# Attention weights on one Trainium2 core: turned tiles in two buffers with transfers of their own

## The chip, the cores and the metric

The kernel runs on one core of one Trainium2 chip. The times are device microseconds (us). The core's engines work beside each other, each through its own instructions in order: TensorE (PE in the profile, its weight loads PEld) multiplies matrices, VectorE (DVE), ScalarE (ACT) and GpSimd (POOL) work on elements, and SyncE (SP) issues the transfers (DMAs) of this stage. They wait for one another through semaphores.

## The reference

The input is 16 sequences of 512 tokens of width 256, in float32. Three layers follow one another, each added to its input: half of a feed-forward block with experts, a causal attention of 16 heads with rotary positions, and half of the same feed-forward block again. The change is in the attention:

```python
q = _rope(q.reshape(b, s, H, DQK).transpose(0, 2, 1, 3))
k = _rope(k.reshape(b, s, H, DQK).transpose(0, 2, 1, 3))
scores = jnp.einsum('bhqd,bhkd->bhqk', q, k) * (1.0 / np.sqrt(DQK))
scores = jnp.where(causal[None, None], scores, -jnp.inf)
probs = jax.nn.softmax(scores, axis=-1)
out = jnp.einsum('bhqk,bhkd->bhqd', probs, v)
return out.transpose(0, 2, 1, 3).reshape(b, s, H * DV) @ Wo + bo
```

A head has 64 columns in q, k and v.

## The kernel before

**Units.** A unit is one sequence and one group of four heads (`HG`): 16 x 4 = 64 units, in this order. The loop over `u` (L1207) is a pipeline over units: in one turn it makes the sums and the output projection of unit `u`, finishes the weights of unit `u + 1` (`old`), makes scores and exponentials of unit `u + 2` (`new`), and the queries and keys of unit `u + 3`.

**Tiles.** The 512 tokens are four tiles of 128. Scores are causal, so tile i of the queries has i + 1 blocks of 128 keys: ten blocks a head. `place` (L1020) says where they lie: tile 3 (four blocks) and tile 2 (three) in one buffer `pr0`, tiles 1 and 0 (two and one) in `pr1`.

**From scores to sums.** `scores` (L1038) lets TensorE fill one PSUM bank a head. `exps` (L1061) takes a head and a tile at a time: VectorE masks and finds the row minimum of the negated scores (L1073), ScalarE takes the exponential and the row sum (L1077). `scaled` (L1080) takes the reciprocal on VectorE and multiplies on GpSimd (L1085). Now the weights have queries on the partitions, and the sums over keys need keys there. So each 128x128 block is turned in two steps. First `turn` (L1088) transposes its sixteen 32x32 squares on VectorE from `pr` into `sq` (L1100); `turn_most(j)` does the three first key blocks of tiles 3 and 2 for head j, `turn_corner` the last block of tile 3 for all heads, `turn_tile(1)` and `turn_tile(0)` the other two tiles. Then `move` (L1119) carries the squares to other partitions: for each quarter of 32 partitions that is a source (`q`) and each that is a target (`k`) one transfer, 16 in all, from `sq` to `prT` (L1127), issued on SP. Each is 32 partitions x 5120 bytes. `sums` (L1149) multiplies: for two heads side by side and for each key tile t one matmul a head over all query tiles i >= t at once (L1158). To make that one contiguous piece, `first` (L1019) gives the place of the first block of each key tile. ScalarE copies the result out of PSUM with the bias (L1169), `leave` (L1171) projects it (L1176), and VectorE adds it to the stream (L1182).

**Order.** Within the attention the instructions of VectorE, ScalarE, GpSimd and SP, and of TensorE in the whole kernel, run in the order in which the program names them; nothing rearranges them. `sq`, `prT`, `pr0`, `pr1` and the values `v` have one buffer each, so a unit writes one only after the unit before has been read. PSUM has eight banks, given out in turn. In one turn of the loop VectorE's order is: reciprocals of tiles 1 and 0, `turn_most(1)`, `turn_most(2)`, more reciprocals, `turn_most(3)`, the corner, tile 1, tile 3 of `new` for head 0, tile 0 (and then SP's 16 transfers), the rest of tiles 3 and 2, the addition to the stream, the rotation of queries and keys (L994), `turn_most(0)` of `new`, and tiles 1 and 0 of `new`.

**Other transfers on SP.** Once per sequence (four units) a sequence that comes later is normalized, its squares turned on VectorE (L961), stored to memory as `away` (L964), and loaded back in two times eight transfers (`land`, L970), which stand at the start of a turn, ahead of the `move`. At the fourth head group the output of a sequence is stored (L1184).

**First and last unit.** Unit 0 and unit 63 are turned by TensorE instead (`turn_at_once`, L1129).

## Time and profile before

| | us |
|---|---|
| median of 3 runs (2309.47 to 2314.15) | 2309.89 |
| profiled execution, its own time | 2317.09 |
| span of its instructions | 2315.4 |
| PE busy | 2254.7 (97%) |
| DVE busy | 1761.6 (76%) |
| ACT busy | 1158.1 (50%) |
| POOL busy | 1068.6 (46%) |

The granted clock of TensorE was 0.995 of full speed in the profiled execution. The attention runs from about 449 us to 1925 us of the span; before and after it the feed-forward blocks run.

How the rows are read: a group of instructions has its line of the kernel, engine and operation, the tile that it writes and those that it reads, the shape, how many there were, busy time and mean length in ns, and the idle time of the engine just before them with what ended it. A row of waits has who waited, for whom, the total, how many times and the longest. A row of one line's instructions has minimum, median and maximum length in ns. A row of the timeline has start, length, engine, line, operation and count.

### The profile page before, as it was taken

The numbers are of one execution on the slowest core, as the hardware profiler recorded it, in microseconds if no ns is written. First come the engines' busy times: TensorE is split into PE (matmuls) and PEld (weight loads), VectorE is DVE, ScalarE is ACT, GpSimd is POOL, SyncE is SP. The second block draws the span as 40 slices with busy tenths as digits, with TensorE's granted clock in tenths as the row PEclk, the third lists the DMA queues.
The fourth block names the chain that finished last, engine by engine and source line by source line (L and its number), as shares of the span: only waits on it lengthen the run. The fifth ranks groups of instructions, "written<-read, shape, count | busy, mean of one in ns | idle before, by whom it ended". The sixth has DMA issues, their size and how long they took to land. (4 is left out here: it accounts for less than half of the span.)

```text
span 2315.4 us, 52884 instructions
## 1 busy us (share of the span) xinstructions
PE 2254.7 (97%) x19544; PEld 1488.2 (64%) x19544; DVE 1761.6 (76%) x4678; ACT 1158.1 (50%) x3296; POOL 1068.6 (46%) x1695
## 2 busy tenths in 40 slices
PE   7999999999999999999999999999999999998999
PEld 4764488566666666666666666666666666764588
DVE  5742298788889898989898988989888875432387
ACT  5753243455555555556464545555555555532233
POOL 2210054565566556565656565656556542210043
PEclk9999999999999999999999999999999999999999
DMA  6839851055556465554655554646455543739734
GB/s 209 261 112 403 339 140 55 7 131 121 130 127 147 110 148 130 122 140 111 146 129 129 128 140 111 158 97 160 120 132 130 124 115 112 237 138 404 305 116 140
DMA packets 221929, 359.52 MB, mean 155 GB/s; under 512 B 99876, under 2 KB 159848, under 8 KB 213480
## 3 DMA queue, kind: packets, MB, share of 16 engines
q1 hardware_dynamic: 220812, 355.34, 55.3%
q8 instruction: 155, 2.54, 0.5%
q14 instruction: 102, 0.84, 0.1%
q10 hardware_dynamic: 860, 0.81, 0.1%
HBM read 156.29 MB, written 37.22 MB: 84 GB/s over the span
## 5 line engine op out<-in xcount | busy, mean ns | idle before, releaser
L1085 POOL TENSOR_SCALAR pr<-pr,ars 128x512 f32<-128x512 f32 (+3 forms) x1024 | 524.1, 532 | 575.0 <-DVE ars L1082 573.8
L1077 ACT ACTIVATE pr<-pr,amn 128x512 f32<-128x512 f32 (+3 forms) x1024 | 561.8, 550 | 219.6 <-DVE amn L1073 215.2
L1100 DVE STREAM_TRANSPOSE sq<-pr 128x768 f32<-128x768 f32 x434 | 384.5, 918 | 130.1 <-DMA prT<-sq 106.7
L1073 DVE CUSTOM_DVE_ANT_0 pr<-p_as,causal 128x512 f32<-128x512 f32 (+2 forms) x768 | 308.6, 457 | 7.0 <-PE p_as L1054 5.8
L1054 PE MATMUL p_as<-k,q 32*64 32x448 f32 (+3 forms) x8192 | 307.3, 414 | 0.0
L1158 PE MATMUL p_av<-prT,v 128*64 128x512 f32 (+3 forms) x2048 | 291.5, 437 | 10.1 <-ACT pr L1077 2.0
L1013 ACT COPY v<-p_v 128x512 f32<-128x512 f32 x128 | 74.6, 585 | 451.3 <-PE p_v L1010 451.3
L1158 PEld LDWEIGHTS p_av<-prT,v 128*64 128x64 f32 x2048 | 161.1, 137 | 139.6 <-issue 92.7
L1176 PE MATMUL p_ay<-wo,aoT 128*128 128x256 f32 x1024 | 238.6, 386 | 4.1 <-DVE amn L1073 3.0
L1010 PE MATMUL p_v<-wv,ahT 128*128 128x256 f32 x1024 | 231.6, 379 | 0.7 <-DVE x L1182 0.7
L988 PE MATMUL p_q<-ahT,wq 128*128 128x512 f32 x512 | 230.6, 593 | 0.2 <-ACT ahT L949 0.2
L1054 PEld LDWEIGHTS p_as<-k,q 32*64 32x64 f32 x8192 | 201.8, 131 | 45.0 <-issue 26.2
L988 PE MATMUL p_k<-ahT,wk 128*128 128x512 f32 x512 | 230.3, 592 | 0.0
L1176 PEld LDWEIGHTS p_ay<-wo,aoT 128*128 128x128 f32 x1024 | 189.2, 190 | 62.2 <-DVE amn L1073 37.0
L1010 PEld LDWEIGHTS p_v<-wv,ahT 128*128 128x128 f32 x1024 | 194.5, 190 | 53.8 <-issue 23.7
L1077 ACT ACTIVATION_READ_ACCUMULATOR pr<-pr,amn 128x1 f32 x1024 | 192.0, 187 | 0.0
L988 PEld LDWEIGHTS p_k<-ahT,wk 128*128 128x128 f32 x512 | 97.3, 190 | 122.0 <-issue 106.9
L988 PEld LDWEIGHTS p_q<-ahT,wq 128*128 128x128 f32 x512 | 97.0, 190 | 95.7 <-issue 78.6
L1073 DVE CUSTOM_DVE_ANT_1 pr<-p_as,causal 128x384 f32<-128x384 f32 x256 | 130.2, 546 | 0.0
L1169 ACT ACTIVATE aoT<-p_av,bcol 128x128 f32<-128x128 f32 (+1 forms) x384 | 117.1, 391 | 9.9 <-PE p_av L1158 9.9
L584 PE MATMUL p_ds<-hT,qk 128*128 128x512 f32 x256 | 118.8, 609 | 2.1 <-ACT hT L159 2.1
L811 PE MATMUL p_cy<-vw,catT 128*128 128x256 f32 x512 | 120.8, 379 | 0.0
(179 smaller groups left out, 3358.0 us busy)
## 6 DMA issues: line engine op xcount, KB each, us to landing
prT<-sq SPq DMA_DIRECT2D x992, 160.0 KB
w<-in_e_W_dram SPq DMA_DIRECT2D x64, 1024.0 KB
w<-in_e_Wg_dram SPq DMA_DIRECT2D x32, 1024.0 KB
out_dram<-x SPq DMA_DIRECT2D x64, 256.0 KB
awaya<-sqa SPq DMA_DIRECT2D x25, 512.0 KB
atT<-awaya SPq DMA_DIRECT2D x100, 128.0 KB
xl<-in_attn_x_dram SPq DMA_DIRECT2D x16, 512.0 KB
xl<-out_dram SPq DMA_DIRECT2D x16, 512.0 KB
```

The source lines that it names most:

```text
L584: nc.tensor.matmul(psc, qk[:, k, c * P:(c + 1) * P], hT[:, k, :], start=(k == 0), stop=(k == NC - 1))
L811: nc.tensor.matmul(py[:, t * D:(t + 1) * D], atT[:, c, t * P:(t + 1) * P], vws[b][:, c, :], start=(c == 0), stop=(c == NC - 1))
L988: nc.tensor.matmul(pq, self.w[:, k, at:at + P], hTs[self.b][:, k, :], start=(k == 0), stop=(k == NC - 1))
L1010: nc.tensor.matmul(pv[:, t * 256:(t + 1) * 256], hTs[b][:, k, (t0 + t) * P:(t0 + t + 1) * P], wv[:, k, hg * HG * DQ:(hg + 1) * HG * DQ], s ...
L1054: nc.tensor.matmul(banks[j][half * H:(half + 1) * H, at:at + wh], q[n][rows, q0:q0 + H], k[n][rows, :wh], start=(n == 0), stop=(n == 1))
L1073: nc.vector.tensor_tensor_reduce(out=by_block(self.at(i, j)), in0=by_block(banks[j][:, at:at + w]), in1=mask(i), scale=-1.0 / math.sqrt(DQ ...
L1077: nc.scalar.activation(self.at(i, j), self.at(i, j), AF.Exp, bias=self.mn[:, i, j:j + 1], scale=-1.0, accum_out=self.rs[:, i, j:j + 1])
L1085: nc.gpsimd.tensor_scalar(self.at(i, j), self.at(i, j), self.rs[:, i, j:j + 1], 1.0, ALU.mult, ALU.mult)
L1100: nc.vector.transpose(view(self.sq, j * blocks * SQ + dst[0] * SQ, [(blocks * SQ, nh)] + [(s * SQ, n) for s, (_, n) in zip(dst[1:], of)] + ...
L1158: nc.tensor.matmul(po[j * DQ:(j + 1) * DQ, :].rearrange("d (a f) -> d a f", a=NSQ)[:, :, t * SQ:], vs[u][:, t, head * DQ:(head + 1) * DQ], ...
L1169: nc.scalar.activation(dst[:, odd, to], src[:, odd, of], AF.Identity, bias=bcol[:, r:r + 1])
L1176: nc.tensor.matmul(py[:, t * D:(t + 1) * D], oTs[u][:, pair, (t0 + t) * P:(t0 + t + 1) * P], wo[:, hg * (HG // 2) + pair, :], start=(pair ...
```

## The change

The turned weights lie in two buffers, as the weights before turning do: `sq0` and `prT0` for tiles 3 and 2 (seven blocks a head), `sq1` and `prT1` for tiles 1 and 0 (three blocks). Each has a `move` of its own of 16 transfers: 32 partitions x 3584 bytes, and 32 partitions x 1536 bytes. The space is the same in all. Three further things go with it:

- Within a `move` the target quarters come in the order 0, 2, 1, 3 in place of 0, 1, 2, 3.
- All of `turn_most` and the corner of a unit stand one turn of the loop earlier than three of the four and the corner did, ahead of the exponentials of its tiles 1 and 0; `move(0)` stands at the start of the next turn, ahead of the scaling of tiles 1 and 0. `turn_tile(1)`, `turn_tile(0)` and `move(1)` come behind tile 3 of `new` for heads 0 and 1.
- `sums` has six pieces in place of four: for key tile t the queries of tiles 3 and 2 from the first buffer (t = 0 to 3), and then those of tiles 1 and 0 from the second (t = 0 and 1). The columns are the same in all.

```diff
-        blocks = NT * (NT + 1) // 2
-        first = [0, 4, 8, 7]
+        blocks = (7, 3)
+        where = ([(2, 0), (3, 0), (2, 1), (3, 1), (2, 2), (3, 2), (3, 3)], [(0, 0), (1, 0), (1, 1)])
+        pieces = [(0, t, max(t, 2), NT - max(t, 2)) for t in range(NT)] + [(1, t, t, 2 - t) for t in range(2)]
...
-                if heads[0] == 0 and which == 0 and len(of) == 2:
-                    self.sq = ap.tile([P, NSQ, HG, blocks * SQ], F32, tag="sq", name=f"sq{self.nm}")
+                n = blocks[which] * SQ
+                if self.sq[which] is None:
+                    self.sq[which] = ap.tile([P, NSQ, HG, n], F32, tag=f"sq{which}", name=f"sq{which}_{self.nm}")
...
-            def move(self):
-                prT = prTs[self.u] = ap.tile([P, NSQ, HG, blocks * SQ], F32, tag="prT", name=f"prT{self.nm}")
+            def targets(self, tag, which):
+                if which == 0:
+                    prTs[self.u] = [None, None]
+                n = blocks[which] * SQ
+                prT = prTs[self.u][which] = ap.tile([P, NSQ, HG, n], F32, tag=f"{tag}{which}",
+                                                    name=f"prT{which}_{self.nm}")
+                return prT
+
+            def move(self, which):
+                prT, sq = self.targets("prT", which), self.sq[which]
                 for n in range(NSQ):
-                    for k in range(NSQ):
+                    for k in (0, 2, 1, 3):
                         q = (k + n) % NSQ
-                        nc.sync.dma_start(prT[k * SQ:(k + 1) * SQ, q, :, :], self.sq[q * SQ:(q + 1) * SQ, k, :, :])
+                        nc.sync.dma_start(prT[k * SQ:(k + 1) * SQ, q, :, :], sq[q * SQ:(q + 1) * SQ, k, :, :])
...
-            for t in range(NT):
-                n = NT - t
+            for one, (which, t, i, n) in enumerate(pieces):
+                at = where[which].index((i, t))
                 for j in range(2):
                     head = pair * 2 + j
                     nc.tensor.matmul(
-                        po[j * DQ:(j + 1) * DQ, :].rearrange("d (a f) -> d a f", a=NSQ)[:, :, t * SQ:],
+                        po[j * DQ:(j + 1) * DQ, :].rearrange("d (a f) -> d a f", a=NSQ)[:, :, i * SQ:(i + n) * SQ],
                         vs[u][:, t, head * DQ:(head + 1) * DQ],
-                        prTs[u][:, :, head, first[t] * SQ:(first[t] + n) * SQ],
-                        start=(t == 0), stop=(t == NT - 1))
+                        prTs[u][which][:, :, head, at * SQ:(at + n) * SQ],
+                        start=(one == 0), stop=(one == len(pieces) - 1))
...
                 elif old:
+                    old.move(0)
                     old.scaled((1, 0), slice(0, HG // 2))
-                    old.turn_most(1)
-                    old.turn_most(2)
                     old.scaled((1, 0), slice(HG // 2, HG))
-                    old.turn_most(3)
-                    old.turn_corner()
-                    old.turn_tile(1)
                 if new:
                     new.scores((3,))
                     new.scores((2,))
-                    new.exps((3,), slice(0, 1))
+                    new.exps((3,), slice(0, 2))
                 if old and 0 <= u < nu - 2:
+                    old.turn_tile(1)
                     old.turn_tile(0)
-                    old.move()
-                if new:
-                    new.exps((3,), slice(1, 2))
+                    old.move(1)
...
                     new.scores((1, 0))
                     if u + 3 < nu:
-                        new.turn_most(0)
+                        for j in range(HG):
+                            new.turn_most(j)
+                        new.turn_corner()
                     new.exps((1, 0))
```

`turn_at_once` (units 0 and 63) fills both buffers in the same way, with the same ten PSUM banks.

More of the change, by code (lines that the diff above doesn't have):

```diff
@@ L1030, in __init__ @@
                 self.rs = small.tile([P, NT, HG], F32, tag="ars", name=f"ars{self.nm}")
-                self.pr = [None, None]
+                self.pr, self.sq = [None, None], [None, None]
                 self.banks = {}
@@ L1088, in turn @@
             def turn(self, which, heads, of, src, dst):
-                if heads[0] == 0 and which == 0 and len(of) == 2:
-                    self.sq = ap.tile([P, NSQ, HG, blocks * SQ], F32, tag="sq", name=f"sq{self.nm}")
-                pr = self.pr[which]
+                n = blocks[which] * SQ
+                if self.sq[which] is None:
+                    self.sq[which] = ap.tile([P, NSQ, HG, n], F32, tag=f"sq{which}", name=f"sq{which}_{self.nm}")
+                pr, sq = self.pr[which], self.sq[which]
                 def view(x, at, dims):
@@ L1098, in turn @@
                 j, nh = heads
-                step = (7, 3)[which] * P
+                step = blocks[which] * P
                 nc.vector.transpose(
-                    view(self.sq, j * blocks * SQ + dst[0] * SQ,
-                         [(blocks * SQ, nh)] + [(s * SQ, n) for s, (_, n) in zip(dst[1:], of)]
-                         + [(HG * blocks * SQ, NSQ), (1, SQ)]),
+                    view(sq, j * n + dst[0] * SQ,
+                         [(n, nh)] + [(s * SQ, m) for s, (_, m) in zip(dst[1:], of)]
+                         + [(HG * n, NSQ), (1, SQ)]),
                     view(pr, j * step + src * P,
@@ L1107, in turn_most @@
             def turn_most(self, j):
-                self.turn(0, (j, 1), [(3, 2), (1, 3)], 0, (2, 1, 3))
+                self.turn(0, (j, 1), [(3, 2), (1, 3)], 0, (0, 1, 2))
             def turn_corner(self):
-                self.turn(0, (0, HG), [], 6, (first[3],))
+                self.turn(0, (0, HG), [], 6, (6,))
             def turn_tile(self, i):
                 if i:
-                    self.turn(1, (0, HG), [(1, 2)], 1, (1, 3))
+                    self.turn(1, (0, HG), [(1, 2)], 1, (1, 1))
@@ L1129, in turn_at_once @@
             def turn_at_once(self, tag, vector):
-                prT = prTs[self.u] = ap.tile([P, NSQ, HG, blocks * SQ], F32, tag=tag, name=f"prT{self.nm}")
-                where = {first[t] + i - t: (i, t) for i in range(NT) for t in range(i + 1)}
-                per = S // P
-                for g in range(HG * blocks // per):
-                    pt = ps(f"p_prT{self.nm}_{g}")
-                    for n in range(per):
-                        j, at = divmod(g * per + n, blocks)
-                        i, t = where[at]
-                        nc.tensor.transpose(pt[:, n * P:(n + 1) * P], self.at(i, j)[:, t * P:(t + 1) * P], ident)
-                    dst = prT.rearrange("p a h f -> p a (h f)")[:, :, g * per * SQ:(g + 1) * per * SQ]
-                    dst = dst.rearrange("p a (n x) -> p a n x", n=per)
-                    src = pt.rearrange("p (n a x) -> p a n x", n=per, a=NSQ)
-                    if g in vector:
-                        nc.vector.tensor_copy(dst, src)
-                    else:
-                        nc.scalar.copy(dst, src)
+                per, done = S // P, 0
@@ new lines, in turn_at_once @@
+                for which in range(2):
+                    prT = self.targets(tag, which)
+                    for g in range(HG * blocks[which] // per):
+                        pt = ps(f"p_prT{self.nm}_{done}")
+                        for n in range(per):
+                            j, at = divmod(g * per + n, blocks[which])
+                            i, t = where[which][at]
+                            nc.tensor.transpose(pt[:, n * P:(n + 1) * P], self.at(i, j)[:, t * P:(t + 1) * P], ident)
+                        dst = prT.rearrange("p a h f -> p a (h f)")[:, :, g * per * SQ:(g + 1) * per * SQ]
+                        dst = dst.rearrange("p a (n x) -> p a n x", n=per)
+                        src = pt.rearrange("p (n a x) -> p a n x", n=per, a=NSQ)
+                        if done in vector:
+                            nc.vector.tensor_copy(dst, src)
+                        else:
+                            nc.scalar.copy(dst, src)
+                        done += 1
```

## The prediction

> **What bounds the kernel now.** I read the page's busy shares and groups first, then the waits, then one line's issues, then the timeline of one unit.

> ```profile
> PE 2254.7 (97%) x19544; PEld 1488.2 (64%) x19544; DVE 1761.6 (76%) x4678; ACT 1158.1 (50%) x3296; POOL 1068.6 (46%) x1695
> ...
> L1100 DVE STREAM_TRANSPOSE sq<-pr 128x768 f32<-128x768 f32 x434 | 384.5, 918 | 130.1 <-DMA prT<-sq 106.7
> ...
> L1158 PE MATMUL p_av<-prT,v 128*64 128x512 f32 (+3 forms) x2048 | 291.5, 437 | 10.1 <-ACT pr L1077 2.0
> ```

> TensorE is the bound. The wait that the change is aimed at is VectorE's: 106.7 us in 52 waits, because the turn of head 0 (L1100) may not overwrite `sq` before the transfers of the unit before have read it.

> One line's issues, on the queue SP:

> ```profile
> L1127 SPq DMA_DIRECT2D prT<-sq x992: 507/590/1704, 460.3 to 1899.5; - x199
> L970 SPq DMA_DIRECT2D ahT<-away x224: 303/449/1736, 546.9 to 1787.1; - x112
> ```

> Issuing one transfer holds SP for 590 ns at the median. A unit has 16 of them (992 in 62 units).

> The timeline of one unit, by engine (start, length, then the work; S is the start of its sums, 1038.93):

> ```profile
> 1038.93 4.53 PE L1158 MATMUL p_av<-prT,v 128*64 128x512 f32 x32
> 1043.39 0.22 PE L1047 MATMUL p_as<-blank 32*64 32x64 bf16 x4
> ...
> 1045.18 0.21 PE L1047 MATMUL p_as<-blank 32*64 32x64 bf16 x3
> ...
> 1046.46 3.72 PE L1176 MATMUL p_ay<-wo,aoT 128*128 128x256 f32 x16
> ```

> ```profile
> 1033.92 5.37 SPq L970 DMA_DIRECT2D ahT<-away  x8
> 1047.09 10.05 SPq L1127 DMA_DIRECT2D prT<-sq  x16
> ```

> ```profile
> 1037.65 0.98 DVE L1100 STREAM_TRANSPOSE sq<-pr 128x768 f32<-128x768 f32 x1 [2.05 <-DMA prT<-sq]
> 1038.78 0.42 DVE L1073 CUSTOM_DVE_ANT_0 pr<-p_as,causal 128x256 f32<-128x256 f32 x1
> ...
> 1041.30 1.80 DVE L1100 STREAM_TRANSPOSE sq<-pr 128x768 f32<-128x768 f32 x2
> ...
> 1043.08 2.73 DVE L1100 STREAM_TRANSPOSE sq<-pr 128x768 f32<-128x768 f32 x3
> 1045.73 0.65 DVE L1073 CUSTOM_DVE_ANT_0 pr<-p_as,causal 128x512 f32<-128x512 f32 x1
> ...
> 1046.32 0.71 DVE L1100 STREAM_TRANSPOSE sq<-pr 128x512 f32<-128x512 f32 x1
> ...
> 1058.12 0.75 DVE L994 SCALAR_TENSOR_TENSOR k<-p_k,bcol,cos 128x512 f32<-128x512 f32 x1
> ```

> ```profile
> 1042.83 1.82 ACT L1169 ACTIVATE aoT<-p_av,bcol 128x256 f32<-128x256 f32 x6
> ```

> TensorE's rows touch: sums to S+4.46, scores of tile 3 to S+6.25, of tile 2 to about S+7.5, then the output projection. Unit after unit the shortest period from sums to sums is 23.25 us. The mean from 476.53 (second unit) to 1881.83 is 1405.3/60 = 23.42. So the stalls that this region could lose are 0.17 us a unit, some 10 us over 62 units: 0.4% of the kernel, however long VectorE's wait is. What can be added has no such ceiling.

> **The change part by part.** The sum is made against the profiled execution, 2317.1 us (span 2315.4); that is 7 us above the median of the runs, so a difference is added to 2309.9.

> *The matmuls of the sums.* Sixteen per unit become 24, over the same 1280 columns per pair of heads. In the trace's records the pairs of matmuls (two heads side by side) start 0.430, 0.323, 0.216 and 0.109 us apart for 512, 384, 256 and 128 columns: 0.835 ns a column plus 2 to 3 ns. Each matmul is two instructions, so a unit has eight more pair slots: 8 x 2.5 ns = 0.02 us, 1.3 us in all. The second buffer brings a second set of semaphore waits on TensorE's sequencer. Now one sums has five such instructions of 51 ns, which stand in the gap of 0.25 us ahead of it. The new ones come behind 1.5 us of queued matmuls, so I take nothing; if that cover fails, up to 0.4 us a unit, 25 us.

> *The transfers.* Sixteen of 160 KB become 16 of 112 KB and 16 of 48 KB, on the same queue. The issues run (10.05 - 0.59)/15 = 0.631 us apart. What sets that for a smaller transfer the trace does not show. From above: the same 0.631, or 0.66 with the rare issues of over 1 us that the maximum of 1704 shows. From below: the 449 ns of the 32 KB transfers (L970), 0.49 with the gap between issues. I take 0.631: bytes do not order these rows (32 KB takes 449, and the 512 KB stores on L964 a median of 522), and inside a burst, while the transfers pile up, it stays at 584 to 597.

> [...]

> *The loop that this closes.* Each buffer exists once. The transfers of the next unit into the big buffer may start when the last sums have read it, and those into the small one follow on the queue. The sums stop at their first matmul of the small buffer until the last transfer has landed. From that landing to the next one:
> - TensorE: small pieces of heads 0 and 1, then big pieces of heads 2 and 3: half of 4.46 = 2.23 us.
> - Two semaphore hops, to SP and back, about 0.1 each: 0.2 (the small turn ends at 1047.03, the first issue is at 1047.09).
> - 31 steps of 0.631: 19.6.
> - The last landing: in the bursts of before it comes 2.5 us after the issue for the first transfer and 4.3 for the last (1033.29 to 1037.65). With less data per issue there is no pile, so 2.4.

> Sum 24.4 us against 23.42, so +1.0 a unit, +61 over 62 units. The shorter loop of before (16 issues) closed over VectorE instead, which is why it waited there.

> *What else is on that queue.* Every fourth unit stores a turned width (L964) and two output pieces (L1184) behind the transfers and, at the start of the next unit, ahead of them, waits for the store and issues 8 loads (L970). In the unit at 1015.33 the loads came 4.4 us after the store was issued and took 8 x 0.49 = 4.0. If T is the last transfer's issue, the next unit's would start at T + 4.8 (landing, sums, hops), but now at T + 0.6 + 4.4 + 4.0 = T + 9.0: +4.2. If the store lands without a pile in 2.8 us (the feed-forward part's store, L570, of the same size: an average wait of 59.3/25 = 2.4, and its issue), +2.6. Between these 3.4, 14 times: +48. The 8 loads a unit later fit into the T + 4.8. Transfers: +109 in all.

> *VectorE's order.* Removed: the wait of 2.05. Moved ahead of the exponentials of tiles 1 and 0 (L1073): three more turns and the corner, 1.80 + 0.9 + 0.63 = 3.3 us. Behind them stand, on VectorE, those exponentials; then ScalarE's, and then, in ScalarE's order, the copies out of the sums (L1169), which free the PSUM banks that the scores of tile 2 need (eight banks in turn). From the first of these exponentials to the last copy it is 1038.78 to 1044.65, 5.87 us. After the change VectorE can take tile 3 from S+6.25 on; from there to the end of the keys' rotation it is 1045.73 to 1058.87 = 13.1, with the wide turn of tiles 1 (1.2) and the four turns and the corner (4.3) 18.6: the next exponentials of tiles 1 and 0 start at S+24.8, that is 1.5 after the next sums start, where they started 0.15 before. The copies end at 1.5 + 5.9 = 7.4, where TensorE wants the banks at 6.25: 1.15 late. A stall there puts the next unit off by as much, so two successive stalls share 1.15: 0.58 a unit, less the 0.17 of now: +25, and half of the 1.3 us width turn in 14 units, +9. But a unit that SP has held back by 1.0 or more has that cover: with the loop above, this costs nothing further. If SP were hidden, it is what is left: +35.

> *The order of quarters.* It can only shorten the pile of landings; with issues the slower part, I take nothing. [...]

> Total: 2309.9 + 1.3 + 109 = 2420.

> **The rivals.**
> 1. *Issues shrink with the bytes* (0.49 to 0.56). For it: L970's 449 ns. Against it: the constancy of 590. Then the loop is 2.23 + 0.2 + 31 x 0.52 + 2.4 = 20.9, under 23.25, only the width units still stall (T + 7.4 to T + 9.0 against some T + 7 of slack: up to 2 us, 14 times), and VectorE's order costs its 35: 2335 to 2370.
> 2. *Faster.* One place decides: when the exponentials of tiles 1 and 0 start. If issues shrink so that a pair costs SP what one cost (0.32 each) and these exponentials start no later than S+0.3, both loops hide and the 10 us of stalls go: 2310 + 1 - 10 = 2301. For it: VectorE does lose 2 us of waiting a unit. Against it: 4.3 us of turns stand where 2.05 + 0.98 stood.
> 3. *No change*: the two effects cancel within 5 us; nothing ties them.
> 4. *Heavier*: 0.66 an issue, the semaphore waits uncovered (25), 4.2 per width unit: 31 x 0.029 x 62 = 56 more, and 11: up to 2510.

> **How the numbers follow.** Forecast 0.62, rival 1 0.20, rival 2 0.07, rival 3 0.04, rival 4 0.07. A measurement of this kernel tells about 0.2% (5 us) from none. Slower: 0.62 + 0.20 + 0.07 = 0.89; same 0.04; faster 0.07. The range leaves out rivals 2 and 3 and the far end of 4: from rival 1's 2335 to 2480. The forecast alone, by the landing (2.2 to 2.5: 0.3 x 62 = 19) and the store (2.6 to 4.2), is 2395 to 2450.

> **What would show it.** VectorE's wait for transfers at L1100 nearly gone; 1984 issues on L1127, still near 590 ns; SP's issues filling over 19 us of each unit; TensorE waiting inside the sums, at their fifth piece, for a transfer; unit period 24.4, and 27 to 28 once in four. I am wrong if issues of the small transfers take under 500 ns, or if the sums' second wait is absent; then look at L1047, waiting for L1169.

## The result and the profile after

| | before | after |
|---|---|---|
| median of 4 runs, us | 2311.05 | 2534.74 |
| lowest to highest | 2309.47 to 2314.15 | 2527.77 to 2541.43 |
| profiled execution, its own time | 2317.09 | 2527.77 |
| its span | 2315.4 | 2526.0 |
| granted clock of TensorE | 0.995 | 0.975 |

The ratio is 1.0966, with a 95% interval of 1.0932 to 1.1. The change costs 224 us. The forecast said slower, and was 115 us short; the time lies above its range.

The profile page of the changed kernel, busy shares and groups. The lines have moved: the turn is L1103, the transfers L1138, the matmuls of the sums L1170.

```profile
PE 2310.5 (91%) x20568; PEld 1585.0 (63%) x20568; DVE 1762.4 (70%) x4678; ACT 1165.5 (46%) x3296; POOL 1069.4 (42%) x1695
...
L1170 PE MATMUL p_av<-prT,v 128*64 128x256 f32 (+1 forms) x3072 | 349.3, 383 | 169.8 <-DMA prT<-sq 157.7
...
L1103 DVE STREAM_TRANSPOSE sq<-pr 128x768 f32<-128x768 f32 x434 | 370.4, 908 | 2.7 <-DMA prT<-sq 2.6
```

The wait that the change aims at is gone: VectorE lost 106.7 us to the transfers at the turn, and now 2.6. In its place TensorE, the engine that bounds the kernel, waits 157.7 us for the same transfers inside the sums. The sums' matmuls are busy for 349.3 us against 291.5, though they cover the same columns; that is the halved clock, below.

The changed kernel, the issues of the transfers' line (minimum, median and maximum in ns), and further down who waited for them (us, times):

```profile
L1138 SPq DMA_DIRECT2D prT<-sq x1984: 507/590/2046, 451.5 to 2115.3; - x199
...
  PE p_av L1170: 157.7, 61
```

Twice as many issues, each as long as before: 589 ns at the median for 1536 bytes a partition and 593 for 3584, where 5120 had taken 590. The 61 waits are one a unit.

The timeline of the changed kernel, the queue SP over two units with the turned width between them:

```profile
1073.20 21.72 SPq L1138 DMA_DIRECT2D prT<-sq  x32
1095.02 0.53 SPq L964 DMA_DIRECT2D away<-ahT  x1
1095.66 1.24 SPq L1196 DMA_DIRECT2D out_dram<-x  x2
1098.02 3.79 SPq L970 DMA_DIRECT2D ahT<-away  x8
1101.92 22.07 SPq L1138 DMA_DIRECT2D prT<-sq  x32
1124.03 4.03 SPq L970 DMA_DIRECT2D ahT<-away  x8
1129.27 1.15 SPq L1138 DMA_DIRECT2D prT<-sq  x2
```

SP has little time left. Of the 28.7 us from the start of one row of transfers to the start of the next, 22 are the row's issues, and what stands between the rows is either the width's transfers or the way from the last landing over TensorE back to SP. The same stretch on TensorE:

```profile
1119.94 1.74 PE L1170 MATMUL p_av<-prT,v 128*64 128x256 f32 x16
1125.39 4.50 PE L1170 MATMUL p_av<-prT,v 128*64 128x256 f32 x32 [3.72 <-DMA prT<-sq]
```

The sums do the 16 instructions on the big buffer, and stand for 3.72 us before the first one on the small buffer. Over the whole attention a unit now takes 26.94 us, measured from its first transfer's issue to that of the next unit (mean of 61), where it took 23.44. 61 x 3.50 is 214 of the 224 us.

In the same stretch the trace shows something that no row of before had shown. The changed kernel's windows (us of the window, then busy time and count of PE, PEld, DVE, ACT and POOL, then TensorE's clock, the DMA share and GB/s):

```profile
1119.90:1121.50 1.60, 1.56 (x16) 1.26 (x16) 1.60 (x4) 0.00 (x0) 0.00 (x0) 1.00 0.38 96
1121.50:1125.39 3.89, 0.18 (x4) 0.03 (x1) 2.27 (x17) 3.58 (x16) 1.41 (x4) 0.95 0.22 53
1125.39:1128.40 3.01, 3.01 (x16) 2.05 (x18) 0.18 (x1) 1.03 (x4) 1.84 (x5) 0.50 0.42 65
1128.40:1129.80 1.40, 1.40 (x18) 1.00 (x14) 0.00 (x0) 0.00 (x0) 0.00 (x0) 1.00 0.27 41
```

After the wait TensorE runs at a clock of 0.50, and sixteen instructions take 3.01 us where they took 1.56. In the records the pairs of matmuls start 0.426 us apart there and 0.216 elsewhere. Of the 30 such drops in the trace 21 last 3.41 us and eight 6.83. Over the whole kernel the half clock holds for 129.9 us, before for 23.5. The drops in the attention begin on one fixed grid: their starts lie whole multiples of 3.41 us apart. Of the stretches of this grid at full clock, 24 were followed by a drop, and in each of them TensorE was idle for 2.08 us or more; in the 429 others it was idle for 2.00 us at most. In the run without the width's loads, below, the two figures are 2.02 and 2.01 us. So here a wait of some 2 us halves the clock, if it falls into one such stretch.

### The profile page after: what moved, and what is told of

Read it like the earlier page. It is cut to its first block, busy times and chain, and to the rows that moved or that the text cites. A ratio compares the mean times of both kernels' runs of the same rounds, so it can differ in the third digit from the quotient of the medians.

```text
span 2526.0 us, 56418 instructions
## 1 busy us (share of the span) xinstructions
PE 2310.5 (91%) x20568; PEld 1585.0 (63%) x20568; DVE 1762.4 (70%) x4678; ACT 1165.5 (46%) x3296; POOL 1069.4 (42%) x1695
## 5 line engine op out<-in xcount | busy, mean ns | idle before, releaser
L1170 PE MATMUL p_av<-prT,v 128*64 128x256 f32 (+1 forms) x3072 | 349.3, 383 | 169.8 <-DMA prT<-sq 157.7
L1170 PEld LDWEIGHTS p_av<-prT,v 128*64 128x64 f32 x3072 | 254.7, 152 | 262.3 <-issue 166.4
L1103 DVE STREAM_TRANSPOSE sq<-pr 128x768 f32<-128x768 f32 x434 | 370.4, 908 | 2.7 <-DMA prT<-sq 2.6
L1056 PEld LDWEIGHTS p_as<-k,q 32*64 32x64 f32 x8192 | 206.0, 132 | 44.5 <-issue 25.5
L1010 PEld LDWEIGHTS p_v<-wv,ahT 128*128 128x128 f32 x1024 | 194.6, 190 | 54.3 <-issue 21.5
L1181 ACT ACTIVATE aoT<-p_av,bcol 128x128 f32<-128x128 f32 (+1 forms) x384 | 123.0, 395 | 121.8 <-PE p_av L1170 121.8
L1084 DVE RECIPROCAL ars<-ars 128x4 f32<-128x4 f32 x254 | 44.9, 177 | 118.6 <-ACT pr L1079 106.9
```

What stands on the lines that cost most here:

```text
L1010: nc.tensor.matmul(pv[:, t * 256:(t + 1) * 256], hTs[b][:, k, (t0 + t) * P:(t0 + t + 1) * P], wv[:, k, hg * HG * DQ:(hg + 1) * HG * DQ], s ...
L1056: nc.tensor.matmul(banks[j][half * H:(half + 1) * H, at:at + wh], q[n][rows, q0:q0 + H], k[n][rows, :wh], start=(n == 0), stop=(n == 1))
L1103: nc.vector.transpose(view(sq, j * n + dst[0] * SQ, [(n, nh)] + [(s * SQ, m) for s, (_, m) in zip(dst[1:], of)] + [(HG * n, NSQ), (1, SQ)] ...
L1170: nc.tensor.matmul(po[j * DQ:(j + 1) * DQ, :].rearrange("d (a f) -> d a f", a=NSQ)[:, :, i * SQ:(i + n) * SQ], vs[u][:, t, head * DQ:(head ...
L1181: nc.scalar.activation(dst[:, odd, to], src[:, odd, of], AF.Identity, bias=bcol[:, r:r + 1])
```

## The experiments

Two theories stood at the start. **Theory 1**: the loop "last landing, rest of the sums, next row of 32 issues, landing" sets the pace, and its length is mostly the number of issues. **Rivals**: VectorE's new order is the loss; the bytes are; the width's transfers are; the halved clock is; the order of the target quarters matters.

In the table, "unit" is the mean from first issue to first issue, "row" the mean from a unit's first to its last issue, "gap" the rest (last issue to the next unit's first), all from each kernel's trace. "Half clock" is the time at 0.50 in the whole kernel.

| kernel | median us | unit | row | gap | half clock us |
|---|---|---|---|---|---|
| before | 2311.05 | 23.44 | 9.71 | 13.7 | 23.5 |
| after | 2534.74 | 26.94 | 20.89 | 6.04 | 129.9 |
| half the transfers | 2349.36 | 24.12 | 10.49 | 13.6 | 9.8 |
| half the bytes, one head a pair | 2495.98 | 26.43 | 20.68 | 5.8 | 109.1 |
| sums buffer by buffer | 2446.69 | 25.63 | 20.9 | 4.73 | 88.2 |
| no loads of the width | 2476.17 | 26.01 | 20.97 | 5.04 | 59.2 |
| both of the last two | 2358.42 | 24.20 | 20.90 | 3.31 | 11.2 |
| VectorE's order of before | 2541.90 | 27.04 | 20.94 | 6.10 | 157.4 |
| the same, half the transfers | 2302.68 | 23.31 | 10.15 | 13.2 | 20.8 |
| before, quarters 0, 2, 1, 3 | 2302.46 | 23.31 | 9.74 | 13.6 | 14.4 |

**Half the transfers.** The targets are kept over all units (`kept`), so that what isn't written is still there to be read.

```diff
-                for n in range(NSQ):
+                for n in range(NSQ // 2):
                     for k in (0, 2, 1, 3):
```

> The changed kernel with only 8 of the 16 transfers of each buffer; the other half of the turned weights keeps what unit 0 left, so the sums use stale weights there. Theory 1 (SP's serial issues, some 0.67 us each with the long ones, close a loop of 25.5 us a unit): 16 issues a unit hide, the loop is gone, and what is left is VectorE's new order, 23.6 to 24.0 us a unit: 2325 to 2350 us. Rival (the new order on VectorE, with ScalarE's copies and the PSUM banks behind it, is most of the loss): it stays above 2450 us.

Measured: 2349.36 us, ratio 1.0152 (1.0106 to 1.0198). The group of the sums on the page of this run:

```profile
L1175 PE MATMUL p_av<-prT,v 128*64 128x256 f32 (+1 forms) x3072 | 291.0, 345 | 7.7 <-issue 1.4
```

No wait for a transfer is left in the sums, and they are busy for 291.0 us. So some 185 of the 224 us hang on the sixteen further transfers a unit, by their issues or by what they carry; VectorE's order may stand behind the other 38.

**Half the bytes.**

```diff
-  nc.sync.dma_start(prT[k * SQ:(k + 1) * SQ, q, :, :], sq[q * SQ:(q + 1) * SQ, k, :, :])
+  nc.sync.dma_start(prT[k * SQ:(k + 1) * SQ, q, :HG // 2, :], sq[q * SQ:(q + 1) * SQ, k, :HG // 2, :])
```

> The changed kernel with all 32 transfers a unit, each carrying two of the four heads only, so half the bytes; the other two heads keep what unit 0 left. Theory 1 (an issue costs the same whatever it carries): 590 ns an issue at the median still, unit period within 0.4 us of the changed kernel's, 2500 to 2540 us. Rival (the moving of the bytes, or their landing, sets the loop): below 2430 us.

Measured: 2442.31 us (1.0511 to 1.0597), which neither had. The issues stayed at 589 ns at the median, and a row at 20.7 us. But the run changed two things. With heads 2 and 3 never written, the second pair of sums no longer held up the next unit's transfers into the big buffer, so the loop lost a part of its TensorE leg too: the gap is 4.8 us a unit, and 5.8 in the run that follows. It was made again with one head of each pair:

```diff
-  ... prT[k * SQ:(k + 1) * SQ, q, :HG // 2, :] ...
+  ... prT[k * SQ:(k + 1) * SQ, q, 1:HG - 1, :] ...
```

> The changed kernel with all its transfers and issues, but each carries heads 1 and 2 only (one head of each pair of sums), so that the waits of both pairs of sums on both buffers stay; heads 0 and 3 of the turned weights are never written, which leaves that part of the computation out. Theory 1 (the loop of issues is what the change costs, whatever they carry): 2500 to 2535 us, 32 issues in 20.5 to 21 us, each near 590 ns. Rival (bytes matter, the run with heads 0 and 1 was cheaper for its bytes): 2430 to 2460 us.

Measured: 2495.98 us (1.0759 to 1.0822), 4 us below theory 1's range and far from the rival's. The row is 20.68 us against 20.89, and the last transfer lands 1.82 us after its issue instead of 1.94 (medians). Half the bytes in as many transfers is worth 39 us; half the transfers, with half the bytes, was worth 185.

**Sums buffer by buffer.** The big buffer's pieces for both pairs come first, then the small one's, so that the big buffer is free before TensorE waits.

```diff
-                    sums(u, 0)
-                    sums(u, 1)
+            for buffer in range(2):
+                for pair in range(2):
+                    multiply(u, pair, pos[pair], buffer)
```

> The changed kernel with the sums in another order: both pairs of heads from the big buffer first, then both from the small one. Theory 1: the loop loses the leg over TensorE (the big buffer is free 3.1 us after the sums start, whatever the small one does), so a plain unit of 3.2 + 20.9 + 2.2 = 26.3 us meets the small pieces at 23.3 + 3.1 = 26.4 without a wait; what is left is SP's own work, 4 x 21.6 + 11 us for the width transfers in four units, 24.4 us a unit: 2365 to 2400 us. Rival (TensorE waits for transfers however the sums are ordered, as the transfers are late in themselves): above 2470 us.

Measured: 2446.69 us (1.0513 to 1.0632): 88 us better than the changed kernel, between the two expectations. With the leg gone the gap shrank, to 0.7 us in some units, but it stayed at 8.3 to 9.4 us in every fourth, where the store of the width, its landing and eight loads stand between two rows. What I had not seen is that the other units do not make up for this.

**The width's transfers on ScalarE's queue.** In the changed kernel two units of each four are long: that with the store and the first eight loads takes 29.2 us in the mean, the next one, with the other eight, 27.3, the others 25.8. The question is whether SP's queue makes them so.

```diff
-                nc.sync.dma_start(self.mem, hTs[self.b].rearrange("p c s -> p (c s)"))
+                nc.scalar.dma_start(self.mem, hTs[self.b].rearrange("p c s -> p (c s)"))
```

and the same for the loads on L970.

> The changed kernel with the store and the 16 loads of the turned width issued on ScalarE's queue. [...] Rival (the long units come from the transfers sharing the DMA engines, not the queue): no gain above 20 us, 2510 us or more.

Measured: 2561.36 us (1.0965 to 1.1171). The time lies in the rival's range, but it is not shown to be for the rival's reason. ScalarE in this run's timeline:

```profile
1257.75 3.90 ACTq L970 DMA_DIRECT2D ahT<-away  x6
1261.75 0.72 ACT L1079 ACTIVATE pr<-pr,amn 128x512 f32<-128x512 f32 x1 [3.96 <-DVE sq L1103]
```

The exponentials queue behind the loads' issues: 3.90 of the 3.96 us that this one waited are issues, and of ScalarE's waits 99.1 us in all are put down to these loads. SP's row became longer as well, 21.87 us on average: SP stood for 71 us between its issues (5 in the changed kernel), 55 of them for a semaphore that a transfer of ScalarE's had been given, as in the last experiment below. The run moved the cost to a queue that had no room for it; it says nothing on what the width costs on SP.

**No loads of the width.** `land` issues nothing; the rest is as in the changed kernel.

```diff
-                for k in squares:
+                for k in squares[:0]:
```

> The changed kernel without the loads that finish the transposed inputs (16 transfers a trip, 14 trips; that part of the computation is left out), all else as it was. Theory A (both halves of the loads stand in the loop of issues, the second as well, and the long waits halve the clock): units all near 25.3 us, 2425 to 2450 us, time at half clock under 40 us. The prediction's account (the loads of the first half alone cost, 2.8 us in each of 14 units, and those of the second half find room): about 2495 us.

Measured: 2476.17 us (1.0682 to 1.0735). The loads cost 58.6 us: more than the prediction's 48 (its account gave about 2495 here, 19 too many), less than theory A's 85 to 110. All four units of a sequence now take 25.9 to 26.2 us. So the loop itself is 26.0, not 25.3, and the reason is seen unit by unit. In 11 of 52 units TensorE's clock dropped between two rows, and there the gap is 6.0 to 6.3 us in the mean; in the others it is 4.5 to 4.7. Most of these drops follow a row of 21.5 us or more. And a row is long where single issues are: its length goes with what its issues of over 0.9 us took beyond 0.59 (correlation 0.94). Without that excess it is 19.7 us in the mean.

**Both: buffer by buffer, no loads.** The two edits together show whether the row itself, without the leg and without the loads, still holds the kernel back.

> Sums that read the big buffer for both pairs first, and then the small one, without the loads that finish the transposed inputs (that part of the computation is left out). Theory 1 (loop of issues, landing and sums' leg, and the width's loads on top): with the leg and the loads gone the row of 20.9 us and one issue step fit into TensorE's own pace, and what is left is VectorE's order, as with half the transfers: 2340 to 2375 us. Rival (32 transfers a unit cost beyond this loop): 2420 us or more.

Measured: 2358.42 us (1.0183 to 1.0221), inside theory 1's range. TensorE's waits in this run (us in total, times, longest us):

```profile
PE p_av L1168 <- DMA prT<-sq: 9.8, 15, 2.3
```

32 issues a unit fit beside TensorE's own work if nothing else closes the loop: 9.8 us of waits are left of 157.7. This is within 9 us of the run with half the transfers. Of the 224 us, then, the loads are 59, the sums' leg between landing and next row 118 (2476.17 to 2358.42), and 47 are left, of which VectorE's order is looked at below. The parts depend on the order in which they are taken away: with the leg first it is 88 for the leg, and 88 for the loads (2446.69 to 2358.42).

**The halved clock.** The question is whether it is a part of the loss. First, eight matmuls of no use in every unit, at the place where TensorE waits:

```diff
             for pair in range(2):
                 multiply(u, pair, pos[pair], 0)
+                if pair == 0:
+                    for _ in range(FILL):
+                        for j in range(2):
+                            nc.tensor.matmul(pos[1][j * DQ:(j + 1) * DQ, :256], vs[u][:, 0, j * DQ:(j + 1) * DQ],
+                                             prTs[u][0][:, :, 0, :2 * SQ], start=True, stop=True)
                 multiply(u, pair, pos[pair], 1)
```

> The changed kernel with eight matmuls of no use (some 1.7 us) between the big and the small pieces of the first pair of sums, where TensorE waits for the last transfers, so that it isn't idle long enough for its clock to be halved. [...] Rival (the clock only fills time in which TensorE would wait anyway, since SyncE's issues set the pace): half clock falls as well, but the time stays at 2525 to 2545 us.

Measured: 2530.61 us (1.0923 to 1.0967), half clock 61.1 us. The rival's range, but not a clean test: the longest waits, in the units after the width's first loads, were still 3.6 us long in the mean behind the filling, and there the clock still fell. In the other units drops became rare (1 in 39, where there had been 9), but the filling itself made a gap at full clock longer, 4.9 us for 4.6 in the units without loads, so that their mean gap stayed. So the filling was put into those units alone, 18 matmuls.

```diff
-FILL = 4
+FILL = 9
...
-                if pair == 0:
+                if pair == 0 and u + 3 in trips:
```

> The changed kernel with 18 matmuls of no use (some 4.3 us) in TensorE's longest wait, that of the units after the width's first loads, some 5.7 us without them; nothing in the other units. Theory A (the halved clock in those units stretches the sums by some 1.6 us and so holds up the next row of issues): time at half clock falls by some 45 us, the time by 14 x 1.6 = 22 us, to 2505 to 2518 us. Rival (the clock has no part in the time): 2528 to 2540 us.

Measured: 2532.06 us (1.0928 to 1.0981), in the rival's range. TensorE in the timeline of this run, one of these units, with the filling on L1184:

```profile
1110.55 1.73 PE L1169 MATMUL p_av<-prT,v 128*64 128x256 f32 x16 [0.15 <-issue]
1112.08 4.08 PE L1184 MATMUL p_av<-prT,v 128*64 128x256 f32 x36
1117.48 3.03 PE L1169 MATMUL p_av<-prT,v 128*64 128x256 f32 x32 [1.31 <-DMA prT<-sq]
```

Here it did what was meant: the last 32 instructions take 3.03 us, where those of the changed kernel's unit shown above took 4.50, and the mean gap of these units fell from 6.51 to 5.29 us. The time did not fall by the 22 us. In the two units that follow the clock now dropped in 12 cases of 26 instead of 6, and they became 0.5 and 0.6 us longer. Theory A falls as it was put: taking the drop away at one place did not shorten the kernel. The trace shows how the drops came back: TensorE's waits in the two units after a filled one grew from 1.83 and 1.86 us in the mean to 2.27 and 2.09, around the 2 us of idle time from which a drop follows (2.05 us or more in the 20 stretches before a drop in this run, 2.02 at most in the 443 others). What the kernel would take with no drop anywhere is not shown.

**The order of quarters.**

```diff
-                    for k in (0, 2, 1, 3):
+                    for k in range(NSQ):
```

> The changed kernel with the target quarters in the order of before (0, 1, 2, 3). Theory 1 (the pace is set by the issues, and where they go doesn't matter): 2525 to 2545 us, the last landing to TensorE's going on 2.0 to 2.3 us after the last issue. Rival (alternating by half lets the transfers run beside each other): slower by 10 us or more, landing at 2.5 us or later.

Measured: 2535.77 us (1.091 to 1.1003), as the changed kernel. The last transfer's landing comes 1.94 us after its issue in both (medians). The order does nothing here. In the kernel before, alone:

> The kernel before with the target quarters in the order 0, 2, 1, 3, its only change. Theory (where transfers go doesn't matter): 2306 to 2316 us, ratio within 0.3 % of 1. Rival (alternating by half shortens the landing after the last issue, 4.3 us in the kernel before where 2.1 us would do, and VectorE's wait for it): 2290 to 2303 us.

Measured: 2302.46 us, ratio 0.9954 (0.9941 to 0.9967). The rival held. The page of this run:

```profile
PE 2247.1 (98%) x19544; PEld 1488.5 (65%) x19544; DVE 1764.6 (77%) x4678; ACT 1157.9 (50%) x3296; POOL 1069.0 (46%) x1695
...
L1100 DVE STREAM_TRANSPOSE sq<-pr 128x768 f32<-128x768 f32 x434 | 384.6, 919 | 75.5 <-DMA prT<-sq 55.2
```

VectorE's wait for the transfers is halved, 55.2 us for 106.7. The traces show where it comes from. In the kernel before, the time from issue to landing grows along a row, from 2.47 us for the first transfer to 4.24 for the last (medians over 62 units): the transfers pile up. With the quarters in the order 0, 2, 1, 3 it grows from 2.61 to 3.27 only. In the changed kernel nothing piles up in either order (2.2 us along the big row, 1.9 along the small one), so there was nothing to win. The one line of the change that helps was put where it can't. The same order in the width's loads too:

```diff
-                for k in squares:
-                    for a in range(NSQ):
+                for a in range(NSQ):
+                    for k in squares:
...
-                    trips[u + 4].land((0, 1))
+                    trips[u + 4].land((0, 2))
...
-                    trips[u + 3].land((2, 3))
+                    trips[u + 3].land((1, 3))
```

> The kernel before with the alternating order of target quarters in its moves, as in the run before, and in the loads that finish the transposed inputs too (quarters 0 and 2 a unit earlier, 1 and 3 after, source by source). Theory (the wait of VectorE for those loads, 19 us, shrinks as that for the moves did): 2290 to 2300 us. Rival (32-KB loads are paced by their issue, not by where they go): 2300 to 2305 us.

Measured: 2301.61 us, ratio 0.9953 (0.9936 to 0.9969): not to be told from the run before. VectorE's wait that the profile puts down to these loads is 22.3 us, and was 19.4. The order made a difference where transfers pile up, and these do not: in the run before, the last of eight loads landed sooner after its issue than the first (1.91 us for 2.34 in the first eight, 2.01 for 3.01 in the second, medians).

**VectorE's order.** Two buffers and 32 transfers, but the turns at their old places:

```diff
                 elif old:
-                    old.move(0)
                     old.scaled((1, 0), slice(0, HG // 2))
+                    old.turn_most(1)
+                    old.turn_most(2)
                     old.scaled((1, 0), slice(HG // 2, HG))
+                    old.turn_most(3)
+                    old.turn_corner()
+                    old.move(0)
+                    old.turn_tile(1)
...
-                        for j in range(HG):
-                            new.turn_most(j)
-                        new.turn_corner()
+                        new.turn_most(0)
```

> The two buffers and the 32 transfers of the changed kernel, but the turns on VectorE and their place among the exponentials as before. Theory 1 (32 issues a unit are the loss, in any order on VectorE): the issues can't begin until the turns that stand after the sums are done, so 20.9 us of issues and 2.1 us of landing follow some 5.4 us of sums' pieces and turns, a period of 28.4 us or more against 23.4: 2580 to 2650 us, slower than the changed kernel. Rival (the new order on VectorE is the loss): below 2400 us.

Measured: 2541.90 us (1.0949 to 1.1011), not to be told from the changed kernel, and 38 us below my range. The gap is 6.10 us as there, and VectorE waits only 18.0 us for transfers: the turns are done beside the row of small transfers, and do not stand in the loop as I had put them. And with half the transfers:

> The same with 16 transfers a unit in place of 32 (half of the turned weights, target tiles kept over the units, that part of the computation left out), beside the run of half the transfers in the changed kernel's order, 2349 us. Theory (what that run still lost, 35 us, is VectorE's new order): 2305 to 2325 us. Rival (it is the split itself: more waits, eight more matmuls a unit): 2340 to 2360 us.

Measured: 2302.68 us, ratio 0.9956 (0.9942 to 0.997). Beside the 2349.36 of the same transfers in the new order this makes VectorE's new order, with the places of the moves that go with it, a loss of 47 us where SP is not the bound, and nothing where it is.

**The small transfers on ScalarE's queue.**

```diff
-  nc.sync.dma_start(prT[k * SQ:(k + 1) * SQ, q, :, :], ...)
+  (nc.sync, nc.scalar)[which].dma_start(prT[k * SQ:(k + 1) * SQ, q, :, :], ...)
```

> The changed kernel with the small buffer's 16 issues on ScalarE's queue, the big one's on SyncE's. Theory 1 (the length of one queue's row of issues is the loss): SyncE's row falls to some 10.3 us, 9.5 us of issues come onto ScalarE, which is busy for 12 of 26 us a unit but then starts exponentials late: 2360 to 2450 us. Rival (issues of two queues slow each other, as SyncE's seemed to beside the width's loads on ScalarE's queue, or ScalarE becomes the bound): issues on both over 0.7 us, 2500 us or more.

Measured: 2939.17 us (1.2689 to 1.2729), the slowest of all. The two queues in this run's timeline, SP first, ScalarE's in the second fence:

```profile
1260.25 18.71 SPq L1138 DMA_DIRECT2D prT<-sq  x16
```

```profile
1267.89 10.99 ACTq L1138 DMA_DIRECT2D prT<-sq  x16
1278.93 0.72 ACT L1079 ACTIVATE pr<-pr,amn 128x512 f32<-128x512 f32 x1 [11.57 <-DMA prT<-sq]
```

Two things happen. ScalarE's exponentials wait for the issues, 680.9 us in all. And SP's row of 16, which took 9.7 us in the kernel before, takes 18.2 on average, though SP's median issue is 512 ns: SP stands between its issues. Their operands say for what: eight semaphores are given out in turn to the transfers of both queues, and from its ninth issue on SP waits for one (100, 103, 106 and so on) that a transfer of ScalarE's has just been given; it went on 1.9 to 2.6 us after that issue, which is about a landing. Such waits come to 574 us. So the program ties the queues together, and the run doesn't say whether they could issue beside each other if it did not.

## Why the prediction was right and wrong

*What bounds the kernel, and the ceiling of the gain.* Right. The prediction put what this region could give at some 10 us. Two kernels that take these stalls away in different ways gained 10.8 and 11.0 us against the runs of before beside them (2302.68 and 2302.46 against 2313.5).

*The matmuls of the sums, +1.3 us and the second set of waits hidden.* Not contradicted. With half the transfers, at full clock, 3072 of them were busy for 291.0 us, where 2048 took 291.5 before.

*0.631 us an issue whatever the size.* Right that the size of a transfer does not set it: medians of 589 to 593 ns from 768 to 5120 bytes a partition. Rival 1 fell with that.

*The loop, 24.4 us a unit, +61.* This is the step that failed, in its size. It is there as described (the first wait at the fifth piece of the sums, and 118 us gained by cutting the sums' leg out of it), but without the width's loads it measures 26.0 us. The term "31 steps of 0.631: 19.6" was mis-sized: the row is 20.9 to 21.0. The step had been read from one unit's row of 10.05 us, and that unit had no long issue. In the kernel before 20 issues of 992 took over 0.9 us, and what they took beyond 0.59 is 0.22 us a unit; in the changed one it was 81 of 1984, and 1.22 us a unit. The prediction had the row before it (the maximum of 1704 ns) and used it only for its upper bound of 0.66; the mean step became 0.674. All rows of before together give 0.648, or 20.1 us for 31 steps: that would have found 0.5 of the 1.4 us that were missing in the row. The rest of the tail came with the change, and not with the fuller queue alone: with half the transfers 44 and 43 of 992 issues were long, in the new order and in the old. The other terms came out near what was forecast together: landing, hops and leg 4.83 forecast, 4.5 to 4.7 measured in the mean in the units at full clock and about 6 where the clock drops, 5.04 over all. Two errors cancel in that: the last landing took 1.94 for 2.4, the hops and the leg some 0.2 more than forecast. So of the 1.6 us a unit 1.4 are the row and 0.2 the other terms, drops included, and 1.6 us over 62 units is 99 of the 115 us that were missing.

*The width's transfers, +48.* Measured 58.6 by leaving the loads out, and 88 where the leg had been cut first. The unit with the store and the first eight loads has a gap of 8.26 us against 4.9 to 5.0, +3.3 where 3.4 was forecast. (The row of eight loads that the prediction read as 4.0 us had taken 4.85; all 28 rows of before took 4.37 in the mean.) "The 8 loads a unit later fit" was the wrong half: that unit's gap is 6.51, +1.6. It is the unit in which TensorE waited long for a row that began late, 5.0 us in the mean; all 13 such units that were counted have the halved clock.

*VectorE's order: nothing while SP holds the unit back, +35 if SP were hidden.* Right in both. The order of before made no difference with 32 transfers; with 16 the new order stood at +35 against the runs of before beside it (2349.36 against 2314.77) and +47 against its like, and the prediction's working (0.58 a unit and 9 us, 45 before the 10 us of stalls that go) lies beside that.

*The order of quarters: nothing.* Right for the change, but for a reason that the prediction saw only half. It said that the order "can only shorten the pile of landings", and did not ask what that pile costs in the kernel before, where it was worth 11 us: in the piled-up row of before the last landing came 1 us sooner, 3.27 us after its issue for 4.24.

*The rivals.* "Heavier", up to 2510, was the nearest, and had the chance of 0.07. Of its three parts the longer issue came true (0.674 for its 0.66), the width's part did not (3.3 us for its 4.2), and uncovered waits on semaphores are not shown. It lacked the clock's drop.

## What to carry to other kernels

Before a buffer is split so that a wait goes away, count what the split adds on the queue that issues it, and ask which loop then closes: here one wait off the path was exchanged for one on it. Read the price of a step from all its occurrences and not from a clean one, look at its tail, and ask what falls into the queue's free time now: a row that fills its queue meets what a half-empty one lets pass (here 81 issues of over 0.9 us, where there had been 20). And try each part of a change alone: the smallest one, an order of four numbers, was a gain of 0.46% in the kernel that was to be replaced.
